# Graph attention, two layers on one core: the order of each layer's last scores, and rows requested in halves

## The chip, the cores and the metric

The kernel runs on one core of one Trainium2 chip. The metric is the device time of one execution in microseconds (us); lower is better. Before the change three runs took 2653.32 to 2656.51 us, with a median of 2653.38.

## The reference

The input is x (128 graphs, 64 nodes each, 768 features) and a 0/1 adjacency for each graph. Rows are normalised and rectified, and then go through two layers of graph attention, each with three 768 x 768 weights:

```python
m_left = jnp.einsum('bsh,oh->bso', h, W_left[l])
m_right = jnp.einsum('bsh,oh->bso', h, W_right[l])
u_left = jnp.einsum('bih,bjh->bij', h, m_left) / temper
u_right = jnp.einsum('bih,bjh->bij', h, m_right) / temper
u = u_left * adj_tri + u_left * diag_mask + u_right * jnp.swapaxes(adj_tri, 1, 2)
delta_exp_u = jnp.exp(u) * adj
attention = delta_exp_u / (jnp.sum(delta_exp_u, axis=2, keepdims=True) + 1e-10)
h_lin = jnp.einsum('bsh,oh->bso', h, W_lin[l]) + b_lin[l]
ctx = jnp.matmul(attention, h_lin)
h = jax.nn.relu(_layer_norm(ctx, ln_a[l], ln_b[l]))
```

After the second layer the input x is added. All of it is in float32.

## The kernel before

**Passes.** Each layer has two passes over all tokens. Pass one (`pass_one`, from L655) makes the attention and leaves it in DRAM; pass two (`pass_two`, from L1012) makes `h_lin`, the context and the norm. The texts below say "first layer" for l = 0 and "second layer" for l = 1.

**Blocks, parts, supers.** 512 tokens (8 graphs) are a block, 256 tokens a part. There are 16 blocks and 32 parts. `SUPER` (L172) groups the parts: a first super of two and then ten supers of three. A super's hidden states lie transposed in `HT`, one tile `ht` for each part: 128 partitions, `C` = 6 chunks of features, 256 tokens.

**Products.** From the second super on (in the second layer from the first), the left and right products of a super are made with a fast scheme of 40 products in place of 54: `PRODUCTS` (L116) names for each the sum of weights and the sum of tokens that enter. POOL makes the sums of tokens (class `Tokens`), DVE and POOL the sums of weights. A product is 8 recorded matmuls into one PSUM bank (C, D, X, Y, Z, V in rotation, four chains at a time). `READS` (L122) lists which outputs each product adds to, with its factor. The function `reads` (L904) issues these additions from the bank into the tiles `M` in SBUF: ACT for the first addition of an output, DVE for all others, the lines "m<-m,X" (L245) and L914 of the profile. There are 18 outputs. Output o belongs to part o // 6 of the super, to the left or right side (o // 3 % 2), and to the chunk pair o % 3 (chunks 0 and 1, 2 and 3, or 4 and 5). The last product, number 39, adds to the outputs 0, 4, 5, 6, 7 and 13. So outputs 0, 4 and 5 (part 0), 6 and 7 (part 1: left side, chunks 0 to 3) and 13 (part 2: left side, chunks 2 and 3) become final last.

**Scores.** `scores(k)` (L722) multiplies `ht` with `M` into the PSUM tile `sc`. For each of the super's six groups of two graphs (q; part q // 2) and each chunk c there are four matmuls, which the profile records twice each: 8 for each (q, c), 288 for a super. They are the line L733. Scores of super k - 1 are issued after the fourth product of super k (L925). Only the last super's scores have no products behind them: at the end of pass one (L936 to L947) the kernel issues the first step of the softmax (POOL), opens the banks of pass two's first groups 0, 1, 3 and 5 (`fresh`, with copies of the bias by ACT, L995), issues groups 0 and 1 (`multiply`, L1006), then the last scores, groups 3 and 5, and the softmax's next steps (`chain`, L737, which read the whole of `sc`). In the scores q runs outermost and c inside, so part 0 comes first.

**Memory shared across passes.** Pass two's tiles take the memory of pass one's. In the second layer parts 0 and 1 of `M` are one tile, and pass two's `a`, `b` (rows of the norm's weights) and its first `hl` (the output of groups) lie over it.

**The planner.** Python functions are put into a plan by slot (`put`, L67); a product is two slots, and `run` issues what is due in the middle and at the end of each product. What is planned is thus issued in order of slots on each engine's queue. `prepare(b, slot)` (L850) plans a block's rows in the first layer: four statistics at slots +1 to +7, the scale at +9, four norms (ACT, in place) at +11 to +17, four DVE transposes from the rows `x` to `xb` at +19, +21, +23 and +25 (L465), and at +27 the store of `xb` to DRAM by four DMAs on SP (L461, "h<-xb"). `end` is +28. There the next block's rows are requested (`load_rows`, L344, the DMAs "x<-in_x_dram" of L361): eight DMAs of 192 KB on SP into two tiles `x`, one for row groups 0 and 1 and one for 2 and 3. Behind them the `ht` loads of the block's two parts follow (L368), each held by a memset on DVE (L367) until the tile's earlier part is done with. Block 4's `prepare` begins at slot 118, so its store is at slot 145 and the request at 146; super 2's products begin at slot 152. In pass one of the second layer the rows come from DRAM where pass two of the first left them.

**SP's queue.** Stores, row requests, `ht` loads and the softmax's stores (L778) all go through SP in the order in which they are issued, and an instruction that waits holds those behind it. The adjacency goes through ACT's queue.

Of the kernel before, what the change touches and what calls it, by code (L numbers as in the profile page):

```python
# [17 lines left out]
def kernel(  # L18
# [12 lines left out]
    nc = tc.nc  # L31
    B, S, H = x.shape
    L = w_lin.shape[0]
    P = 128
    C = H // P
# [3 lines left out]
    PAIR = P // S  # L39
# [18 lines left out]
    PB = TH // S  # L58
# [8 lines left out]
    def put(slot, *fs):  # L67
        plan.setdefault(slot, []).extend(fs)

    def put_all(slot, fs, step=1):  # L70
        for f in fs:
            if f is not None:
                put(slot, f)
            slot += step
        return slot
# [5 lines left out]
    def run(slot):  # L81
# [34 lines left out]
    PRODUCTS = (  # L116
# [57 lines left out]
    PLAIN = 36  # L174
    SCORED = 3

    def begins(k, l=0):
        return 0 if k == 0 else 2 * (len(PRODUCTS) if l else PLAIN) + 2 * len(PRODUCTS) * (k - 1)

# [160 lines left out]
    XR = {}  # L340

    START = (0, 2, 1, 3)

    def load_rows(l, u, pool):  # L344

        XR[l, u] = []
        if (l, u) == (0, 0):

            rows = x.rearrange("(n k h) s f -> n k (h s) f", k=Q, h=PAIR)
            for g in range(2):  # L350
                t = pool.tile([P, 2, H], F32, name="x", bufs=2)
                XR[l, u].extend([t[:, 0, :], t[:, 1, :]])
            for q in START:
                nc.sync.dma_start(XR[l, u][q], rows[0, q])
            return
        for g in range(2):
            t = pool[g] if type(pool) is list else pool.tile([P, 2, H], F32, name="x", bufs=2)
            for a in range(4):
                i = 4 * g + a
                src = x[u * NBB + i] if l == 0 else ROWS[u][i]  # L360
                nc.sync.dma_start(t[a * 32:(a + 1) * 32], src.rearrange("(k j) h -> j k h", k=2))  # L361
            XR[l, u].extend([t[:, 0, :], t[:, 1, :]])

    def load_part(which, l, p, hold=False):
        ht = HT[which, l, p] = big.tile([P, C, TH], F32, name="ht", bufs=6)
        if hold:
            nc.vector.memset(ht[:, 0, :1], 0.0)  # L367
        nc.sync.dma_start(ht, KEPT[l][p])  # L368
# [5 lines left out]
    def affine_part(which, l, p, step=1):  # L374

        def part(c0):
            for c in range(c0, c0 + step):
                ht = HT[which, l, p][:, c, :]
                nc.scalar.activation(ht, ht, AF.Relu, bias=cols[1][:, c:c + 1], scale=cols[0][:, c:c + 1])  # L379

        return [lambda c=c: part(c) for c in range(0, C if l else 0, step)]
# [273 lines left out]
    def pass_one(l, start, final):  # L655
        with tc.tile_pool(name=f"one{l}", bufs=2, reuse_waits="tile") as sp, \
# [22 lines left out]
            if l:  # L679
                both = sp.tile([P, 2, C, PB, 2, S], F32, name="m", bufs=1)  # L680
                M = [both[:, 0], both[:, 1]]
                both = both.rearrange("p v c b k s -> p (v c b k s)").rearrange(
                    "p (c b k s) -> p c b k s", c=C, b=2 * PB, k=2)
# [25 lines left out]
            def out_of(bank, thirds=False, o=0):  # L709
                if thirds:  # L710
                    p = bank[:, :4 * CUT].rearrange("p (g b s) -> p g b s", g=2, s=WIDE)
                    return p[:, :, :, THIRDS[o // 6][1]:]
                return bank.rearrange("p (g b s) -> p g b s", g=2, s=S)
# [8 lines left out]
            def scores(k):  # L722
                nq = 2 * len(SUPER[k])
                p = KEEP["scores"].rearrange("p a (q m) -> p (a q) m", m=P)
                for q in range(nq):
                    ht, m = HT[1, l, SUPER[k][q // 2]], M[q // 2]
                    for c in range(C):
                        for h in range(PAIR):
                            b = q % 2 * PAIR + h
                            mb = both[:, c, q // 2 * PB + b] if l and k == 0 else m[:, c, b]  # L730
                            mb = mb.rearrange("p k j -> p (k j)")
                            for e in (0, 32):
                                nc.tensor.matmul(p[h * S + e:h * S + e + 32, q, e:e + 95],  # L733
                                                 ht[:, c, b * S + e:b * S + e + 32], mb[:, e:e + 95],
                                                 start=(c == 0), stop=(c == C - 1))

            def chain(k):  # L737
                adj, nq = ADJ[k], 2 * len(SUPER[k])
# [42 lines left out]
            def softmax(k):  # L781
                CHAIN[k] = chain(k)
                return [lambda: next(CHAIN[k], None)] * 8

            mid = None
            if l == 0:
# [5 lines left out]
                p = ps_st.tile([P, 2 * TH], F32, name="V")  # L792
# [6 lines left out]
                todo, turns = transpose_rows(0, 0, sp)  # L799
# [22 lines left out]
            def bank_of(n):  # L822
                n %= BANKS
                return KEEP["CD"][n] if n < 2 else KEEP["XYZV"[n - 2]]
# [25 lines left out]
            def prepare(b, slot, step=1):  # L850
                if (l, b) not in XR:
                    load_rows(l, b, sp)
                end = put_all(slot + 1, [f for f in transpose_rows(l, b, sp) if step > 1 or f is not None], 1)
                if b + 1 < NB and (l, b + 1) not in XR:
                    put(end + (8 if b == 2 else 0), lambda: load_rows(l, b + 1, sp))
                for t in range(2):
                    p = 2 * b + t
                    k = where[p][0]
                    before = p - 6
                    at = end + 3 + t  # L860
                    lag = 22 if b > 2 else 30 if l else 16
                    if before >= 0:
                        at = max(at, begins(where[before][0] + 1, l) + 2 * SCORED + 3)
                    put(at, lambda p=p, hold=before >= 0: load_part(1, l, p, hold))
                    put_all(at + lag + 6 * t, affine_part(1, l, p))
                    follow.setdefault(k, []).append(at + lag + (7 + 6 * t if l else 0))
                    if len(follow[k]) == len(SUPER[k]):
                        tokens.ready[k] = max(follow[k])
# [25 lines left out]
            last = len(SUPER) - 1  # L894
            for k in range(FIRST_OF[l], len(SUPER)):
                assert slot == begins(k, l)
                if k:
                    put_all(slot + 2 * SCORED + 4, softmax(k - 1), 3)
                    put(slot + 2 * SCORED + 42, lambda k=k: load_adj(k, nc.scalar))
                if k == last:  # L900
                    final(slot, tokens)
                seen, waiting = set(), []

                def reads(i):  # L904
                    for o, c in READS[i]:
                        bank = out_of(bank_of(CHAINS * (k - 1) + i % CHAINS), k == 0, o)
                        to = into(o, k == 0)
                        if o not in seen:
                            seen.add(o)
                            nc.scalar.activation(to, bank, AF.Copy, scale=float(c))  # L910
                        elif abs(c) == 1:
                            added(nc.vector, to, "+" if c > 0 else "-", to, bank)
                        else:
                            nc.vector.scalar_tensor_tensor(to, bank, float(c), to, op0=ALU.mult, op1=ALU.add)  # L914

                for i, (f, t) in enumerate(PRODUCTS):
                    while l and f not in weights.at:
                        fetch.popleft()()
                    w, tok = weights.need(f), tokens.need(k, t)
                    product(bank_of(CHAINS * (k - 1) + i % CHAINS), w, tok, i < CHAINS, slot, TH if k else 2 * CUT)  # L920
                    tokens.used(k, t)
                    if k == last:
                        weights.used(f)
                    waiting.append(i)
                    if i == SCORED and k:  # L925
                        scores(k - 1)
                    if i >= SCORED or k == 0:
                        for n in waiting:
                            reads(n)
                        waiting = []  # L930
                    turn_of(slot + 1)
                    slot += 2
# [432 lines left out]
```

## Time and profile before

| what | value |
|---|---|
| runs | 2653.32, 2653.38, 2656.51 us |
| the profiled execution's own time | 2651.07 us |
| its span, first to last instruction | 2649.3 us |
| mean granted TensorE clock | 0.995 |
| DVE busy | 1776.2 us (67%) |
| POOL busy | 1764.6 us (67%) |
| moved by DMA | 331.84 MB, mean 125 GB/s |
| code fetched for TensorE's queue (q8) | 145 packets, 2.38 MB |

The span is the time from the first to the last instruction; the execution's own time includes what lies around it. PE is TensorE's matmuls, PEld its weight loads, DVE VectorE, ACT ScalarE, POOL GpSimd and SP the engine that issues most DMAs. In a timeline a row gives start, length, engine, line, operation, output<-input, shapes and count, and in brackets the idle time ahead of it with what ended it. "issue" there means that the engine waited for nothing that the profile shows. The passes lie as follows: pass one of the first layer up to 860 us, pass two up to some 1340, pass one of the second layer up to 2158, pass two to the end.

### The profile page before, as it was taken

What the parts mean: (1) busy time and instruction counts of PE and PEld (TensorE: products, weight loads), DVE (VectorE), ACT (ScalarE), POOL (GpSimd) and SP (SyncE); (2) the same over time, 40 slices, a digit from 0 to 9 for tenths busy, and PEclk for the clock granted to TensorE, in tenths of its full rate; (3) what the DMA queues carried; (4) which work ended last, traced back from release to release, by engine and by line L of the source; (5) the groups of instructions that cost most, each with busy time, mean ns of one, the idle gap of its engine ahead of it and who ended that gap; (6) DMA issues with size and microseconds to landing.
All of it is one profiled execution on the core that took longest, in us unless ns stands there. A gap on an engine that the chain in (4) does not pass through costs nothing. (4 is left out here: it accounts for less than half of the span.)

```text
span 2649.3 us, 47197 instructions
## 1 busy us (share of the span) xinstructions
PE 2593.0 (98%) x18122; PEld 2216.7 (84%) x18122; DVE 1776.2 (67%) x2884; ACT 935.3 (35%) x1969; POOL 1764.6 (67%) x1396
## 2 busy tenths in 40 slices
PE   9899999999999999999999999999999999999998
PEld 8788888888888788888788888888888878888876
DVE  7877878777867445554446676677766676666667
ACT  5522123222213254454542222222222335555453
POOL 4766666656668657776266666667666657878786
PEclk9999999999999999999999999999999999999999
DMA  7443534343321344445794524353542215555555
GB/s 219 113 111 81 129 93 104 92 126 79 89 62 63 123 145 152 163 134 179 212 291 100 131 58 112 78 129 93 133 101 70 67 49 157 157 167 166 176 160 147
DMA packets 258465, 331.84 MB, mean 125 GB/s; under 512 B 56002, under 2 KB 190402, under 8 KB 258242
## 3 DMA queue, kind: packets, MB, share of 16 engines
q1 hardware_dynamic: 241442, 320.56, 44.1%
q10 hardware_dynamic: 16800, 8.26, 1.1%
q8 instruction: 145, 2.38, 0.4%
q14 instruction: 78, 0.64, 0.1%
HBM read 213.39 MB, written 115.34 MB: 124 GB/s over the span
## 5 line engine op out<-in xcount | busy, mean ns | idle before, releaser
L245 POOL TENSOR_TENSOR g<-ht 128x512 f32<-128x512 f32 (+1 forms) x620 | 785.4, 1278 | 424.3 <-PE X L702 82.1
L245 POOL TENSOR_TENSOR g<-g,g 128x512 f32<-128x512 f32 (+1 forms) x310 | 397.6, 1290 | 134.4 <-PE C L702 22.3
L245 POOL TENSOR_TENSOR g<-ht,g 128x512 f32<-128x512 f32 (+1 forms) x272 | 346.1, 1282 | 164.5 <-PE Z L702 43.9
L702 PE MATMUL X<-g,g 128*128 128x256 f32 (+1 forms) x1080 | 251.6, 376 | 2.5 <-POOL g L245 1.2
L702 PE MATMUL C<-g,g 128*128 128x256 f32 x1008 | 242.9, 384 | 9.2 <-POOL g L245 7.1
L1006 PE MATMUL Z<-g,g 128*128 128x256 f32 x1024 | 244.2, 380 | 3.8 <-ACT hl L300 3.6
L702 PE MATMUL Y<-g,g 128*128 128x256 f32 (+1 forms) x968 | 226.8, 377 | 4.4 <-POOL g L245 4.4
L702 PEld LDWEIGHTS X<-g,g 128*128 128x128 f32 x1080 | 201.5, 190 | 31.4 <-POOL g L245 2.5
L702 PEld LDWEIGHTS C<-g,g 128*128 128x128 f32 x1008 | 192.6, 192 | 38.0 <-issue 7.1
L1006 PEld LDWEIGHTS Z<-g,g 128*128 128x128 f32 x1024 | 191.6, 190 | 36.4 <-issue 4.1
L379 ACT ACTIVATE ht<-ht,b_col,a_col 128x256 f32<-128x256 f32 x384 | 196.1, 591 | 67.2 <-DMA ht<-h 42.5
L702 PE MATMUL Z<-g,g 128*128 128x256 f32 (+1 forms) x936 | 217.2, 375 | 0.0
L702 PE MATMUL D<-g,g 128*128 128x256 f32 x880 | 209.1, 381 | 0.6 <-POOL g L245 0.6
L702 PEld LDWEIGHTS Y<-g,g 128*128 128x128 f32 x968 | 182.7, 191 | 28.8 <-POOL g L245 4.8
L702 PE MATMUL V<-g,g 128*128 128x256 f32 (+1 forms) x840 | 193.8, 373 | 3.6 <-DVE m L245 2.0
L702 PEld LDWEIGHTS Z<-g,g 128*128 128x128 f32 x936 | 174.7, 190 | 23.2 <-issue 0.3
L702 PEld LDWEIGHTS D<-g,g 128*128 128x128 f32 x880 | 168.0, 191 | 24.7 <-POOL g L245 1.3
L1006 PE MATMUL X<-g,g 128*128 128x256 f32 x768 | 182.7, 379 | 0.0
L702 PEld LDWEIGHTS V<-g,g 128*128 128x128 f32 x840 | 156.9, 190 | 23.8 <-DVE m L245 2.2
L1206 POOL TENSOR_TENSOR z<-z,b 128x768 f32<-128x768 f32 x62 | 112.6, 1828 | 82.1 <-DVE z L1203 77.5
L245 DVE TENSOR_TENSOR m<-m,D 128x512 f32<-128x512 f32 x180 | 118.2, 677 | 70.5 <-ACT m L910 51.8
L245 DVE TENSOR_TENSOR m<-m,Y 128x512 f32<-128x512 f32 (+2 forms) x196 | 126.4, 666 | 57.9 <-ACT m L910 35.6
(222 smaller groups left out, 4607.8 us busy)
## 6 DMA issues: line engine op xcount, KB each, us to landing
ht<-h SPq DMA_DIRECT2D x126, 768.0 KB, 6.2
h<-xb SPq DMA_DIRECT2D x124, 384.0 KB, 7.0
z<-z SPq DMA_DIRECT2D x128, 192.0 KB, 3.1
x<-z SPq DMA_DIRECT2D x128, 192.0 KB, 5.3
xr<-in_x_dram SPq DMA_DIRECT2D x120, 192.0 KB, 3.8
out_dram<-xr SPq DMA_DIRECT2D x120, 192.0 KB, 2.7
x<-in_x_dram SPq DMA_DIRECT2D x112, 192.0 KB, 5.4
g<-form SPq DMA_DIRECT2D x40, 256.0 KB, 5.1
```

Of the source, the lines that this page charges most:

```text
L245: (eng.tensor_add if sign == "+" else eng.tensor_sub)(o, a, b)
L379: nc.scalar.activation(ht, ht, AF.Relu, bias=cols[1][:, c:c + 1], scale=cols[0][:, c:c + 1])
L702: nc.tensor.matmul(o, w[:, c, g * P:(g + 1) * P], t, start=(new and g == c == at == 0), stop=(c == K2 - 1), skip_group_check=True)
L1006: nc.tensor.matmul(p[:, n], b[t][:, c, r * P:(r + 1) * P], w[s][:, c, :], start=(i in FIRST and i not in PRELOAD and n == c == 0), stop=(c ...
L1206: nc.gpsimd.tensor_add(zs[k], zs[k], rows["b"])
```

## The change

First, where k is the last super, `scores` goes through its (q, c) pairs in the order of a new table `SCORES_LAST`: part 2 with chunks 0, 1, 4, 5; part 1 with 4, 5; part 2 with 2, 3; part 1 with 0 to 3; part 0 with all. As sums of several q are then open in one bank, only the first matmul to a bank and a group of its partitions has the start flag. Second, `reads` of the last super's last product takes its outputs in the order 13, 6, 7, 0, 4, 5 (`LAST_READ`). For other supers the order of scores is the old one. Third, in the first layer `load_rows` for blocks 4 to 15 is called twice: for tile 0 at `end - 5`, which is slot +23, behind the third transpose, and for tile 1 at `end`.

```diff
+    SCORES_LAST = ((2, (0, 1, 4, 5)), (1, (4, 5)), (2, (2, 3)), (1, (0, 1, 2, 3)), (0, tuple(range(C))))
+    LAST_READ = (13, 6, 7, 0, 4, 5)
...
-    def load_rows(l, u, pool):
+    def load_rows(l, u, pool, some=range(2)):
...
-        for g in range(2):
+        for g in some:
...
-                for q in range(nq):
+                todo, begun, left = [(q, c) for q in range(nq) for c in range(C)], set(), {}
+                if k == last:
+                    todo.sort(key=lambda qc: next(n for n, (v, cs) in enumerate(SCORES_LAST)
+                                                  if qc[0] // 2 == v and qc[1] in cs))
+                for q, c in todo:
                     ht, m = HT[1, l, SUPER[k][q // 2]], M[q // 2]
...
+                    left[q] = left.get(q, C) - 1
...
+                            new = (q // 4, h, e) not in begun if k == last else left[q] == C - 1
+                            begun.add((q // 4, h, e))
+                            nc.tensor.matmul(p[h * S + e:h * S + e + 32, q, e:e + 95],
+                                             ht[:, c, b * S + e:b * S + e + 32], mb[:, e:e + 95],
+                                             start=new, stop=not left[q], skip_group_check=k == last)
...
-                    put(end + (8 if b == 2 else 0), lambda: load_rows(l, b + 1, sp))
+                    if l == 0 and b > 2:
+                        put(end - 5, lambda: load_rows(l, b + 1, sp, (0,)))
+                        put(end, lambda: load_rows(l, b + 1, sp, (1,)))
+                    else:
+                        put(end + (8 if b == 2 else 0), lambda: load_rows(l, b + 1, sp))
...
-                    for o, c in READS[i]:
+                    at_end = k == last and i == len(PRODUCTS) - 1
+                    for o, c in sorted(READS[i], key=lambda oc: LAST_READ.index(oc[0])) if at_end else READS[i]:
```

More of the change, by code (lines that the diff above doesn't have):

```diff
@@ L342 @@
     START = (0, 2, 1, 3)
-    def load_rows(l, u, pool):
-        XR[l, u] = []
+    def load_rows(l, u, pool, some=range(2)):
+        XR.setdefault((l, u), [])
         if (l, u) == (0, 0):
@@ L724, in scores @@
                 p = KEEP["scores"].rearrange("p a (q m) -> p (a q) m", m=P)
-                for q in range(nq):
-                    ht, m = HT[1, l, SUPER[k][q // 2]], M[q // 2]
[L727 to L735, printed above, removed]
+                todo, begun, left = [(q, c) for q in range(nq) for c in range(C)], set(), {}
[3 more added lines that the diff above has]
+                for q, c in todo:
+                    ht, m = HT[1, l, SUPER[k][q // 2]], M[q // 2]
+                    left[q] = left.get(q, C) - 1
+                    for h in range(PAIR):
+                        b = q % 2 * PAIR + h
+                        mb = both[:, c, q // 2 * PB + b] if l and k == 0 else m[:, c, b]
+                        mb = mb.rearrange("p k j -> p (k j)")
+                        for e in (0, 32):
+                            new = (q // 4, h, e) not in begun if k == last else left[q] == C - 1
[3 more added lines that the diff above has]
+                                             start=new, stop=not left[q], skip_group_check=k == last)
             def chain(k):
```

## The prediction

> **What bounds the kernel now.** I read the page first, then the waits of TensorE, then the timeline of the places which the change touches.
>
> ```profile
> span 2649.3 us, 47197 instructions
> PE 2593.0 (98%) x18122; PEld 2216.7 (84%) x18122; DVE 1776.2 (67%) x2884; ACT 935.3 (35%) x1969; POOL 1764.6 (67%) x1396
> ```
>
> TensorE is busy for 2593.0 of 2649.3 us. A change that leaves its matmuls alone, as this one does, can save only some of the 56.3 us in which it stands, and time in which it runs slowly. The waits of TensorE from 95 to 790 us, which is the first layer's pass one after its start, have three lines, and those of POOL in the same stretch include one on `ht`:
>
> ```profile
> PE sc L733 <- issue: 5.6, 6, 2.7
> PE sc L733 <- DVE m L245: 2.4, 4, 1.2
> PE C L702 <- ACT m L910: 1.0, 1, 1.0
> ```
> ```profile
> POOL g L245 <- DMA ht<-h: 36.5, 4, 11.4
> ```
>
> Columns: total, times, longest. So almost every stop is inside the score matmuls (`sc`), and most of it is "issue": nothing in the profile is awaited. The measure for a score block that nothing disturbs, between two products:
>
> ```profile
> 324.49 1.89 PE L702 MATMUL Y<-g,g 128*128 128x256 f32 x8
> 326.31 6.31 PE L733 MATMUL sc<-m,ht 128*32 128x95 f32 x288
> 332.55 1.99 PE L702 MATMUL C<-g,g 128*128 128x256 f32 x8
> ```
>
> The scores start 1.82 us after the start of the group ahead of them, and the next group starts 6.24 us later: 21.7 ns for each of 288 recorded matmuls (two for each in the code).
>
> **Part A, the last scores, first layer.** Timeline:
>
> ```profile
> 861.86 1.89 PE L1006 MATMUL V<-g,g 128*128 128x256 f32 x8
> 864.16 2.47 DVE L245 TENSOR_TENSOR m<-m,Y 128x512 f32<-128x512 f32 x4
> 864.89 6.32 PE L733 MATMUL sc<-m,ht 128*32 128x95 f32 x265 [1.14 <-DVE m L245]
> 865.49 0.32 PEld L733 LDWEIGHTS sc<-m,ht 128*32 128x32 f32 x16 [0.28 <-DVE m L245]
> 866.09 4.95 PEld L733 LDWEIGHTS sc<-m,ht 128*32 128x32 f32 x234 [0.28 <-DVE m L245]
> 866.55 0.68 DVE L914 SCALAR_TENSOR_TENSOR m<-Y,m 128x512 f32<-128x512 f32 x1
> 867.15 0.67 DVE L245 TENSOR_TENSOR m<-m,Y 128x512 f32<-128x512 f32 x1
> 867.94 0.59 ACT L995 COPY Y<-g 128x512 f32<-128x512 f32 x1 [3.02 <-DVE m L245]
> 871.85 0.69 PE L733 MATMUL sc<-m,ht 128*32 128x95 f32 x23 [0.64 <-issue]
> 872.47 1.99 PE L1006 MATMUL X<-g,g 128*128 128x256 f32 x8
> ```
>
> DVE adds the last product's six outputs from 864.16 to 867.82, one each 0.6 us, in the order 0, 4, 5, 6, 7, 13. The scores begin with part 0, which needs output 0 at once, 4 sixteen matmuls later and 5 after sixteen more: hence 1.14 and twice 0.28 us.
>
> The change removes no instruction and adds none. In the new order 64 matmuls (part 2, chunks 0, 1, 4, 5) and 32 (part 1, chunks 4, 5) need none of these six outputs, so they can start at 861.86 + 1.82 = 863.68, 1.21 us earlier. Then 13 is wanted at 863.68 + 96 x 0.0217 = 865.76 and is there at 864.83; 6 at 866.46 (865.5), 7 at 866.8 (866.1), 0 at 867.85 (866.7), 4 at 868.2 (867.3), 5 at 868.55 (867.82). The least margin is 0.7 us: no wait on DVE is left. If only that counted, the block would end at 863.68 + 6.24 = 869.92 for 872.47: 2.55 us, the upper bound.
>
> What is late next is "issue". The 0.64 us stop falls after matmul 265. Each matmul has a weight load, so 128 of them are 256 instructions, and stops of this kind in one block lie 128 matmuls apart (second layer: 158 and 286, below). I take them for code that arrives in blocks, each asked for when the block before it is entered. Matmul 137 ran at 866.09 + 105 x 0.0217 = 868.37, and the block after it could go on at 871.85: 3.48 us, against 128 x 0.0217 = 2.78 us that the matmuls need. With the earlier start, matmul 9 runs at 863.88 and 137 then 2.78 to 3.28 us later (3.28 is what it took before, waits included), at 866.66 to 867.16; matmul 265 at 870.14 to 870.64; the next group 0.62 us later, at 870.76 to 871.26. Gain 1.2 to 1.7; I take 1.2, as the code supply had just these gaps.
>
> [...]
>
> **Part A, second layer.**
>
> ```profile
> 2160.19 1.89 PE L1006 MATMUL V<-g,g 128*128 128x256 f32 x8
> 2163.22 4.01 PE L733 MATMUL sc<-m,ht 128*32 128x95 f32 x158 [1.14 <-DVE m L245]
> 2164.42 2.60 PEld L733 LDWEIGHTS sc<-m,ht 128*32 128x32 f32 x126 [0.28 <-DVE m L245]
> 2167.39 2.82 PE L733 MATMUL sc<-m,ht 128*32 128x95 f32 x128 [0.15 <-issue]
> 2170.86 0.35 PE L733 MATMUL sc<-m,ht 128*32 128x95 f32 x2 [0.66 <-issue]
> 2171.14 1.99 PE L1006 MATMUL X<-g,g 128*128 128x256 f32 x8
> ```
>
> Start at 2162.01. Matmul 30 ran at 2164.1, 158 at 2167.39 (3.27 us), 286 at 2170.86 (3.47 us). Now 30 runs at 2162.66, 158 at 2165.93, 286 at 2169.4, the next group at 2169.68: gain 1.46, say 1.5. Without the code limit 2162.01 + 6.24 = 2168.25: 2.9.
>
> Here part 0 shares its memory with tiles that the next pass writes, so the first copies into `hl` and the loads of `a` and `b` must now wait for the end of the scores. These copies (two of some 0.6 us) lie beside the two groups of 1.73 us that follow the scores: no cost, and at most 1.2 us if that cover were gone. The bias copy into Y (867.94 above) still follows the last addition and is 2 us ahead of its group. DVE's softmax begins at the end of the scores as before and moves with it.
>
> Part A: 1.2 + 1.5 = **2.7 us**. From above 2.55 + 2.9 = 5.4; from below nothing, should refills take 0.7 us longer each.
>
> **Part B, rows in two halves.** Twelve requests are split (rows of blocks 4 to 15). I looked at each score block of the first layer for the traffic beside it. One meets rows:
>
> ```profile
> 169.12 4.60 PE L733 MATMUL sc<-m,ht 128*32 128x95 f32 x211
> 176.45 3.32 PE L733 MATMUL sc<-m,ht 128*32 128x95 f32 x77 [2.73 <-issue]
> 179.69 2.19 PE L702 MATMUL Z<-g,g 128*128 128x256 f32 x8
> 181.72 1.89 PE L702 MATMUL V<-g,g 128*128 128x256 f32 x8
> ```
> ```profile
> 157.40 5.15 SPq L461 DMA_DIRECT2D h<-xb  x4
> 162.66 6.84 SPq L361 DMA_DIRECT2D x<-in_x_dram  x8
> ```
> ```profile
> 170.00:174.00 4.00, 3.72 (x179) 3.51 (x170) 0.00 (x0) 1.01 (x3) 0.62 (x1) 1.00 0.98 215
> 176.40:179.70 3.30, 3.25 (x78) 2.91 (x77) 0.00 (x0) 0.00 (x0) 0.00 (x0) 0.55 0.02 5
> ```
>
> The last three columns of the windows are granted clock, DMA share, GB/s. From scores to next group it is 10.57 us here for 6.24: 4.33 lost, of which 2.73 is the stop, and the rest a granted clock of 0.55 after it. The following group takes 2.03 for 1.82: another 0.2. DMA was full up to about 174 with block 4's store and block 5's rows. The code block is in the DMA queues' rows: none from 170 to 173.5, where the data queue is alone, one after that:
>
> ```profile
> q1 hardware_dynamic: 328, 0.81, 103.7%
> ```
> ```profile
> q8 instruction: 1, 0.02, 2.8%
> ```
>
> Its request belongs to matmul 83, at 169.12 + 83 x 0.0217 = 170.9. Code came 5.5 us later, not 3.48.
>
> With the change the first half is issued at slot 141, between transposes. Its tile is free after the second one:
>
> ```profile
> 152.90 0.96 DVE L465 STREAM_TRANSPOSE xb<-x 128x768 f32<-128x768 f32 x1
> ```
>
> So SP issues four requests of 0.855 us (6.84 / 8) from 153.9 to 157.3, ahead of the store at 157.40, which isn't delayed. The rows total 8 x 192 KB; half of them, 0.79 MB at 215 GB/s, is 3.7 us of traffic, moved into a time when SP had issued nothing. DMA then drains at about 170.5, before the code is asked for at 170.9. Code comes at 170.9 + 3.48 = 174.4; natural arrival at matmul 211 is 173.7, so a stop of 0.7 stays, like the 0.64 us above, after which no slow stretch follows. The 77 matmuls take 77 x 0.0217 + 0.14 = 1.8 us: next group at 176.2 for 179.69, 3.5 us, and 0.1 to 0.2 from its speed: **3.6 us**. Bounds: 4.5 (all of it) and nothing.
>
> The other eleven splits I cost at nothing. Each moves four requests past the store of the block's transposed part, and past a softmax's stores where these are near; those come at most 3.4 us later, and the `ht` loads behind them up to 3.4 us earlier. What covers this is POOL's lead: TensorE waited for no POOL sum from 95 to 790 us. Without cover it is the slower rival below. The remaining stops of "issue" there, 5.6 - 2.7 = 2.9 us, bound a further gain; they have no rows beside them, so I take none.
>
> **Sum.** 2.7 + 3.6 = 6.3 us. The profiled execution took 2651.07 us (span 2649.3): 2644.8. The median shown is 2653.38, 2.3 us above it; I forecast against that: **2647.1 us**.
>
> **Rivals.**
>
> *The code block doesn't wait for rows.* If a refill gets its turn between packets, the 2.7 us stop has another cause, and only part A remains: 2653.38 - 2.7 = 2650.7. For it: refill stops of 0.64 and 0.66 us also come with no rows near (the two ends above). Against: the refill packet appears just as the data ends. 0.17. [...]
>
> *Code is no limit.* Both upper bounds: 5.4 + 4.5 = 9.9, 2643.5. Against: 3.3 to 3.5 us per block in both layers. 0.08.
>
> *Part A does not do what it says.* If waits are for whole parts, the scores still start with the first addition (864.89) and stand again for part 1; only the two 0.28 stay, about 1 us in both layers: 2653.38 - 1 - 3.6 = 2648.8. Against: the old order waited chunk by chunk. 0.06.
>
> *Slower: SP held by the early half.* Its request stands at the head of SP's queue until DVE has done two transposes; behind it wait the block's store and its `ht` loads, then POOL's sums, which already waited four times for `ht`. From the point where POOL's lead is under the delay (up to 3.4 us), TensorE stops, and a long stop also slows what follows:
>
> ```profile
> 844.56 2.61 PE L702 MATMUL C<-g,g 128*128 128x256 f32 x8 [2.52 <-POOL g L245]
> 846.97 2.97 PE L702 MATMUL D<-g,g 128*128 128x256 f32 x8
> 849.77 1.89 PE L702 MATMUL X<-g,g 128*128 128x256 f32 x8
> ```
>
> Two groups take 5.21 us for 3.45, with the wait 4.3 us lost. Three such stops in twelve blocks: 12.9 - 6.3 = 6.6 us slower, 2660. Against: no wait for POOL in that stretch. 0.07.
>
> **How the numbers follow.** My forecast has 0.62. A measurement can tell 0.2%, 5.3 us, from no change; the forecast's 6.3 lies just beyond, with some 1.2 us either way from the refill times and the drain, so I give 0.48 of it to faster and 0.14 to same. With the rivals: faster 0.48 + 0.08 = 0.56; same 0.14 + 0.17 + 0.06 = 0.37; slower 0.07. The range runs from the case without code limit, 2643.5, to the case of part A alone with 0.8 us for a worse refill, 2651.5; the slower case is left out.
>
> **What would show it.** Right: no wait on DVE before either last score block, and those blocks 1 to 2 us nearer to the group ahead; in each still one stop of "issue" of 0.6 to 1 us; the stop in the block at 169 us under 1 us, the granted clock 1.0 behind it, and rows drained before 171 us. Wrong: that stop still above 2 us though the rows are gone; a wait of TensorE for POOL or `ht` between 95 and 790 us; new waits of TensorE on `hl` after the last scores.

## The result, and the profile after

Four runs of the changed kernel took 2640.21 to 2644.4 us, with a median of 2642.6; four of the kernel before, on the same chip, 2653.32 to 2657.48, median 2654.95. The ratio is 0.9953, with a 95% interval of 0.9941 to 0.9964: 12.35 us faster by the medians, where 6.3 was forecast. The time is 0.9 us below the range on record. A second comparison on another chip (e4 below) gives 0.9967 [0.9955, 0.998], 9.9 us. The two profiled executions are 7.1 us apart, 2651.07 and 2643.98 us; single runs of one kernel scatter by about 2.5 us (standard deviation).

The head of the page after, and then what TensorE waited for from 95 to 790 us:

```profile
span 2642.2 us, 47249 instructions
PE 2590.5 (98%) x18122; PEld 2216.3 (84%) x18122; DVE 1776.0 (67%) x2884; ACT 934.9 (35%) x1969; POOL 1764.3 (67%) x1396
```
```profile
PE sc L743 <- issue: 3.2, 6, 1.2
PE sc L743 <- DVE m L248: 1.2, 4, 0.3
```

The matmuls are the same 18122. In this stretch "issue" fell from 5.6 to 3.2 us (e3, the kernel before again, has 6.8), and the waits of the scores on DVE from 2.4 to 1.2. TensorE still waits for no POOL sum there.

**The block at 169 us.** TensorE's timeline, SP's queue, and windows (columns as in the prediction: the last three are granted clock, DMA share, GB/s):

```profile
168.75 1.89 PE L705 MATMUL D<-g,g 128*128 128x256 f32 x8
170.57 6.47 PE L743 MATMUL sc<-m,ht 128*32 128x95 f32 x288
176.97 1.99 PE L705 MATMUL Z<-g,g 128*128 128x256 f32 x8
```
```profile
155.34 1.74 SPq L364 DMA_DIRECT2D x<-in_x_dram  x4
158.85 5.17 SPq L464 DMA_DIRECT2D h<-xb  x4
164.12 4.95 SPq L364 DMA_DIRECT2D x<-in_x_dram  x4
```
```profile
168.00:170.50 2.50, 2.50 (x13) 1.98 (x11) 2.50 (x5) 0.00 (x0) 1.89 (x2) 1.00 0.91 244
170.50:174.00 3.50, 3.50 (x169) 3.43 (x172) 0.76 (x2) 0.00 (x0) 1.28 (x1) 1.00 0.33 88
174.00:177.00 3.00, 3.00 (x133) 2.63 (x121) 0.47 (x1) 2.56 (x5) 0.00 (x0) 1.00 0.03 8
```

Four requests now stand ahead of the store and four behind it. DMA is down to a third of its time once the scores run, all 288 matmuls go in one row without a stop, and the clock stays at 1.00. The scores start 1.82 us after the group ahead and the next group 6.40 us later: 0.16 us lost, where it was 4.33.

**The last scores of the first layer, and of the second:**

```profile
857.46 1.89 PE L1021 MATMUL V<-g,g 128*128 128x256 f32 x8
859.28 6.28 PE L743 MATMUL sc<-m,ht 128*32 128x95 f32 x288
865.49 1.99 PE L1021 MATMUL X<-g,g 128*128 128x256 f32 x8
```
```profile
2155.17 1.89 PE L1021 MATMUL V<-g,g 128*128 128x256 f32 x8
2156.99 6.19 PE L743 MATMUL sc<-m,ht 128*32 128x95 f32 x286
2164.11 0.35 PE L743 MATMUL sc<-m,ht 128*32 128x95 f32 x2 [0.93 <-issue]
2164.39 1.99 PE L1021 MATMUL X<-g,g 128*128 128x256 f32 x8
```

No wait on DVE is left in either. The first has no stop of "issue" either; the second keeps one of 0.93 us at matmul 286.

**Where the 7.1 us lie.** I cut both traces at the same matmuls and took the difference of each stretch, after less before: the block at 169 us and the group behind it -4.4; the rest of the first layer's pass one up to its last scores -1.5; these last scores -2.6; the second layer's last scores -1.7; its pass two -0.3. Together -10.5. The other stretches gave +3.4 back (start to 169 us +1.4, the end of the first layer's pass two +1.1, the second layer's pass one up to its last scores +0.8). The 1.4 us lie ahead of 93 us, before the first split request is issued (115.96), the change doesn't touch the work of the other two, and the two profiles of the kernel before (the first and e3) differ from each other by 1.0 and 3.2 us there. Another difference between executions is the clock: up to the last matmul it was granted at 0.50 for 17.1 us before, 23.9 in e3, 13.7 after and 17.1 in e4, in pieces of 3.41 us or multiples. In one such piece TensorE loses up to 1.7 us, half of 3.41.

For the experiments I use one measure: what a score block loses against the undisturbed one of the prediction, that is, the time from the start of the group ahead to the start of the group behind, less 1.82 + 6.24 us. In us, from one profiled execution of each:

| kernel | block at 169 us | other 8, layer one | last, layer one | last, layer two |
|---|---|---|---|---|
| before | 4.33 | 9.08 | 2.55 | 2.89 |
| e3, before again | 4.45 | 10.41 | 2.64 | 3.15 |
| after | 0.16 | 7.64 | -0.03 | 1.16 |
| e4, after again | 0.22 | 9.13 | 0.62 | 1.78 |
| e1, part A alone | 2.77 | 10.14 | 0.30 | 1.53 |
| e2, part B alone | 0.70 | 7.30 | 2.55 | 2.79 |
| e5, one split | 0.64 | 8.66 | 2.48 | 2.95 |
| e6, the other eleven | 2.46 | 8.85 | 2.67 | 3.90 |
| e7, block 5's rows late | 0.47 | 9.92 | 2.54 | 3.44 |
| e8, code shifted | 2.90 | 8.15 | 1.85 | 2.06 |
| e9, order of scores alone | 3.44 | 10.46 | 3.68 | 3.67 |
| e10, order of reads alone | 4.49 | 9.90 | 5.18 | 5.56 |
| e12, after with shift | 0.00 | 5.65 | 0.17 | 0.36 |

### The profile page after: what moved, and what is told of

Read it like the earlier page. It is cut to its first block, busy times and chain, and to the rows that moved or that the text cites. A ratio compares the mean times of both kernels' runs of the same rounds, so it can differ in the third digit from the quotient of the medians.

```text
span 2642.2 us, 47249 instructions
## 1 busy us (share of the span) xinstructions
PE 2590.5 (98%) x18122; PEld 2216.3 (84%) x18122; DVE 1776.0 (67%) x2884; ACT 934.9 (35%) x1969; POOL 1764.3 (67%) x1396
## 4 chain that ended last, share of the span: by engine, by line
PE 86%; DVE 5%; DMA 3%; ACT 2%; issue 1%; POOL 1%; SPq 1%; ACTq 0%; DVEq 0%; POOLq 0%
PE Z L1021 12%; PE C L705 8%; PE Y L705 8%; PE X L705 8%; PE D L705 8%; PE Y L1021 8%; PE Z L705 8%; PE V L705 7%; PE X L1021 6%; PE sc L743 5%; PE V L1021 4%; PE aux L1063 2%; DVE m L248 2%; POOL g L248 1%; DMA g<-form 1%
```

## The experiments

My theory was that of the prediction: the block at 169 us stops because its code waits behind rows, and the last blocks because they wait for DVE and then for code. Rivals: the refill doesn't wait for rows; the excess over the forecast comes from the other eleven splits, or from scatter.

**e1 to e4: the parts alone, and both kernels again.** Runs on one chip, beside 27 runs of the kernel before (median 2652.97, 2649.76 to 2659.08). e1 undoes the split:

```diff
-                    if l == 0 and b > 2:
-                        put(end - 5, lambda: load_rows(l, b + 1, sp, (0,)))
-                        put(end, lambda: load_rows(l, b + 1, sp, (1,)))
-                    else:
-                        put(end + (8 if b == 2 else 0), lambda: load_rows(l, b + 1, sp))
+                    put(end + (8 if b == 2 else 0), lambda: load_rows(l, b + 1, sp))
```

> Part A alone (the order of the last scores and of the last reads), rows requested whole as before. Theory 1 (the two traces: each last score block loses its waits on DVE, and the stop of the code refill gets shorter too, because a refill is no longer asked for late behind a waiting matmul): 4 to 5 us faster than before, 2.6 in the first layer and 2.1 in the second; no wait of TensorE on DVE at either last score block. Theory 2 (my prediction: the code supply keeps its gaps): 2.7 us faster. Theory 3 (the larger gain is run-to-run difference in the stretches that the change does not touch): under 2 us. The stop of 2.7 us in the score block at about 169 us stays in all three.

e2 undoes the order of scores and of reads:

```diff
-                if k == last:
+                if False:
...
-                            new = (q // 4, h, e) not in begun if k == last else left[q] == C - 1
+                            new = left[q] == C - 1
...
-                    at_end = k == last and i == len(PRODUCTS) - 1
+                    at_end = False
```

> Part B alone (rows of blocks 4 to 15 in two halves), scores and reads in the old order. Theory 1: 4.4 us faster, all of it in the score block at about 169 us, whose stop and slow clock go; the last score blocks keep their waits on DVE of 1.14 us and twice 0.28 us. Theory 2 (the other eleven splits help too, as the trace after has shorter stops in the blocks at 250, 403 and 558 us): 6 to 7 us faster. Theory 3 (a refill does not wait for rows): no change, and the stop at 169 us stays.

e3 and e4 are the kernels before and after, without an edit.

> The kernel before, unchanged, for a second profile. All theories: no change in time. What tells them apart: if the stops of 0.6, 0.9 and 1.25 us in the score blocks at 250, 403 and 558 us, the 2.0 us wait at 77 us and the stops at 1356 and 1396 us come back within 0.2 us, they are fixed for this program, and the differences there between before and after belong to the change; if they move by 0.5 us and more, they are differences from run to run. The stop of 2.7 us at 169 us should come back in any case.

> The changed kernel, unchanged, for a second profile and a time on this chip. Theory 1: 9 us faster than before (4.5 from part A, 4.4 from part B), equal to the sum of the two single parts within 1.5 us. Theory 2: 12 us, more than the sum of the parts. In its profile no stop over 0.5 us in the score block at about 170 us, and no wait on DVE at the last score blocks.

Measured: e1 2649.29 us (11 runs), ratio 0.9992 [0.9983, 1.0001], which doesn't exclude no change; e2 2649.71 (11), 0.9984 [0.9975, 0.9992]; e3 2654.02 (11), 1.0002 [0.9994, 1.0011]; e4 2643.09 (5), 0.9967 [0.9955, 0.998]. By means, with standard errors, e1 saves 3.3 +- 1.0 us, e2 4.5 +- 0.9, e4 9.9 +- 1.2. The parts make 7.8; that they are worth 2.1 more together is within these errors. By time alone e1 can't tell 2.7 from 4 us, nor e2 4.4 from 6; the traces have to. The first comparison's 12.35, with four runs a side, is at the high end of the same gain.

In the table each part acts where it was meant to: e1 on the two last blocks, e2 on the block at 169 us. e1's last block, first layer:

```profile
862.26 5.66 PE L743 MATMUL sc<-m,ht 128*32 128x95 f32 x265
868.18 0.69 PE L743 MATMUL sc<-m,ht 128*32 128x95 f32 x23 [0.26 <-issue]
```

The stop is at matmul 265 as before, but 0.26 us for 0.64. It varies between executions of the new order, from nothing (after) to 0.62 lost (e4).

**e5 to e7: whose rows stop the block at 169 us.** All without part A, on one chip, beside 30 runs of the kernel before (2654.09). e5 splits block 5's rows alone, e6 all but those, and e7 is the kernel before with block 5's rows requested 24 slots later, behind the scores:

```diff
# e5
-                    if l == 0 and b > 2:
+                    if l == 0 and b == 4:
# e6
-                    if l == 0 and b > 2:
+                    if l == 0 and b > 2 and b != 4:
# e7
-                    put(end + (8 if b == 2 else 0), lambda: load_rows(l, b + 1, sp))
+                    put(end + (8 if b == 2 else 24 if l == 0 and b == 4 else 0), lambda: load_rows(l, b + 1, sp))
```

> Only the request of block 5's rows (the one beside the score block at 169 us) in two halves; the other eleven and all of part A as before. Theory 1 (three sources of the gain: that score block 3.7 us, the last scores 3.8 us, the other eleven splits about 2 us): the score block at 169 us loses its 2 to 4 us, and nothing else changes: 3 to 4 us faster than before. Theory 2 (my prediction costed the other splits rightly at nothing): this run is as fast as part B alone, 4.5 us.

> The other eleven requests in two halves, block 5's whole, part A as before. Theory 1: the score block at 169 us keeps its stop of 2.6 us or more; the waits on DVE before the score blocks at 403 and 558 us shrink from 0.6 and 1.2 us to 0 and 0.3, because the loads of ht behind the rows come 3.4 us earlier, POOL's sums start earlier, and a small DVE operation in the norm (nb) no longer stands behind a POOL operation of 1.27 us there (1.19 us for 0.24); 1 to 2 us faster in all. Theory 2: no change.

> The kernel before with one edit: block 5's rows requested whole, but 24 slots later (behind the score block at 169 us), so that no rows move while its code is fetched. Theory 1 (the refill waited for the rows): the stop of 2.7 us falls under 1 us, about 3.5 us faster in that block, as with the halves. Rival (a refill does not wait for rows; the halves helped in another way, by the earlier store and ht loads): the stop stays at 2.6 us or more.

Measured: e5 2647.19 us (6 runs), 0.9971 [0.9959, 0.9983]; e6 2652.26 (12), 0.9991 [0.9982, 1.0]; e7 2654.83 (11), 0.9999 [0.999, 1.0009]. The block in e5, e6 and e7:

```profile
171.94 4.60 PE L743 MATMUL sc<-m,ht 128*32 128x95 f32 x211
176.97 1.92 PE L743 MATMUL sc<-m,ht 128*32 128x95 f32 x77 [0.44 <-issue]
```
```profile
168.95 4.60 PE L743 MATMUL sc<-m,ht 128*32 128x95 f32 x211
175.81 1.92 PE L743 MATMUL sc<-m,ht 128*32 128x95 f32 x77 [2.26 <-issue]
```
```profile
170.13 4.60 PE L733 MATMUL sc<-m,ht 128*32 128x95 f32 x211
174.99 1.92 PE L733 MATMUL sc<-m,ht 128*32 128x95 f32 x77 [0.26 <-issue]
```

The same matmul, 211, in all three. With block 5's rows in halves the stop is 0.44 us, with them out of the way altogether 0.26, with them whole 2.26, though the other eleven requests are split. The code's packet shows it too: it begins 4.1 to 5.0 us after the scores' first matmul in the six profiles of unshifted code with these rows whole, 2.2 to 2.6 in the five with them in halves or late. And in all 14 profiles each of the 211 stops of "issue" in the scores ends 2.1 to 3.0 us after the start of a packet of code. So the stops are code, and the rival that a refill doesn't wait for rows falls by the 2.26 against 0.26 us.

e7 saved 3.9 us in this block and gave them back. DVE's waits from 180 to 300 us, TensorE's from 180 to 600, and SP's queue:

```profile
DVE st L336 <- DMA x<-in_x_dram: 5.0, 2, 3.5
```
```profile
PE V L702 <- POOL g L245: 1.4, 1, 1.4
```
```profile
180.58 35.39 SPq L361 DMA_DIRECT2D x<-in_x_dram  x16
```

DVE stands for the rows, and TensorE then for POOL: from the second group behind this block to the end of the stop at 844 us the kernel needs 668.9 us, where the eleven other profiles whose code isn't shifted have 661.3 to 664.3. The edit did more than it was meant to: there are 16 requests in place of 8, since block 5's preparation found no rows and asked as well. So e7 shows that a free block isn't enough if rows come late and SP is held, but not what a late request alone costs.

e5 saves more by its runs, 6.9 +- 1.0 us, than its block does (3.7 in the profile). e5 and e6 together are e2, and their 6.9 + 2.6 on this chip stand against 4.5 +- 0.9 on the other. What the rest is stays open.

**e8: where the stops lie.** The kernel before with 24 transposes more behind the 34 at the start (L793); they compute nothing that is used:

```diff
-                for _ in range(34):
+                for _ in range(58):
```

> The kernel before with 24 more warm-up transposes, which do nothing for the output, at the very start: all later code lies 24 matmuls (48 instructions) further, so blocks of code end 24 matmuls earlier in the program. Theory 1 (the stops called issue are refills of code, and a refill asked for behind a matmul that waits comes late): the stops in all score blocks move 24 matmuls earlier (at the first layer's end from 265 to 241), and there the refill is now asked for ahead of the matmul that waits on DVE, so the stop of 0.64 us after the waits goes and the loss in that block falls from 2.55 to about 1.9 us. Rival (my prediction: blocks of code come at fixed gaps of 3.5 us): the stop moves too, but stays at 0.6 us. Rival 2 (not code): the stops stay at matmul 211, 229 and 265 of their blocks.

Measured: 2649.09 us (8 runs), 0.9983 [0.9972, 0.9995]. The block at 169 us, then the first layer's last block:

```profile
170.23 4.11 PE L733 MATMUL sc<-m,ht 128*32 128x95 f32 x187
177.11 2.32 PE L733 MATMUL sc<-m,ht 128*32 128x95 f32 x101 [2.78 <-issue]
```
```profile
860.61 1.89 PE L1006 MATMUL V<-g,g 128*128 128x256 f32 x8
863.65 6.95 PE L733 MATMUL sc<-m,ht 128*32 128x95 f32 x288 [1.14 <-DVE m L245]
870.52 1.78 PE L1006 MATMUL X<-g,g 128*128 128x256 f32 x7
```

The stop moves from matmul 211 to 187, by exactly the 24 instruction pairs put in: these stops belong to places in the code. It is 2.78 us long here too, behind the same rows. In the last block the stop is gone and the waits on DVE are not, and the loss falls from 2.55 to 1.85: the two are separate costs. Where all of the 5.0 us by which the medians differ come from isn't shown: e8's profile has 8.5 us of "issue" in the scores, the first one before 8.1 and e3 12.8.

**e9 and e10: the halves of part A,** both with whole requests; e9 keeps the old order of reads, e10 the old order of scores (its edits to `scores` are those of e2).

```diff
# e9
-                    at_end = k == last and i == len(PRODUCTS) - 1
+                    at_end = False
# e10
-                if k == last:
+                if False:
```

> Half of part A: the new order of the last scores, the last product's reads in the old order (0, 4, 5, 6, 7, 13), rows whole. Both theories take the order of reads for needed: output 13, now wanted after 96 matmuls, is still the last to be added, 3.7 us after the first addition begins. The scores start 1.2 us earlier and then stand about 2 us for DVE; the last score blocks lose about 2.1 to 2.4 us each, where the old order loses 2.6 and 3.0: at most 1 us faster in all. If the gain of part A came from the scores' order alone, it would be 3.8 us.

> The other half: the last reads in the order 13, 6, 7, 0, 4, 5, the scores in the old order, part 0 first, rows whole. Output 0 comes 1.85 us later than before, and the scores begin with it: each of the last two score blocks starts 1.85 us later and loses about 4 us and more; 3 to 4 us slower than before in all. Rival (the order of reads does not matter): no change.

Measured, beside 21 runs of the kernel before (2653.84): e9 2655.17 us (10 runs), 1.0001 [0.999, 1.0011]; e10 2657.65 (10), 1.0016 [1.0007, 1.0025]. The last block in e9, then in e10:

```profile
865.51 2.17 PE L743 MATMUL sc<-m,ht 128*32 128x95 f32 x96
869.72 5.78 PE L743 MATMUL sc<-m,ht 128*32 128x95 f32 x192 [2.04 <-DVE m L248]
```
```profile
867.12 8.28 PE L743 MATMUL sc<-m,ht 128*32 128x95 f32 x288 [3.13 <-DVE m L248]
```

In e9 the 96 matmuls that need no late output start at once, as the prediction said, and then the scores stand 2.04 us for output 13, which the old order adds last. In e10 the scores stand 3.13 us at once, since output 0 is now added fourth. Neither half gains alone. For e9 2.1 to 2.4 us of loss were expected in these blocks; 3.7 came. There is no stop of code in them; the rest is the clock behind the wait (e9, third last column):

```profile
871.00:874.00 3.00, 3.00 (x85) 3.00 (x80) 0.00 (x0) 0.38 (x1) 0.00 (x0) 0.50 0.00 0
```

It was granted at 0.50 for 3.41 us, and at 0.50 in e10's last blocks too, where the wait is longer still; the waits of 1.14 us in the kernel before are followed by none.

**e11 and e12: two ways to more.** e11 cuts every score block but the last, and that behind the second layer's first super, in two: `scores(k, qs)` makes half of the groups after product 3, with the reads of products 0 and 1 behind them, and the others after product 4. e12 is the changed kernel with e8's 24 transposes.

```diff
# e11
-                        scores(k - 1)
+                            scores(k - 1, (2, 3, 0))
...
+                    if i == SCORED + 1 and k and not (l and k == 1):
+                        scores(k - 1, (1, 4, 5)[:2 * len(SUPER[k - 1]) - 3])
# e12
-                for _ in range(34):
+                for _ in range(58):
```

> The changed kernel, and the scores of every super but the last (and but the first of the second layer) in two pieces of 144 recorded matmuls with one product between them: groups 2, 3, 0, then product 4, then groups 1, 4, 5. Theory 1 (the stops called issue are code refills of about 3.5 us for blocks that 128 score matmuls use up in 2.8): the product gives a refill 1.7 us more, so nearly all stops of issue in these 18 blocks go, 6 to 9 us in sum over the profile; product 4 may wait some 0.2 to 0.3 us each time for ACT's first copies; 3 to 6 us faster than the changed kernel. Rival (not the code supply): the stops stay, and the waits for ACT make it 3 us or more slower than the changed kernel.

> The changed kernel with 24 more warm-up transposes, which do nothing for the output. Theory 1: as in the kernel before, the code blocks end 24 matmuls earlier, which there took 2 to 3 us from the stops of issue and the waits behind them; the changed kernel has lost part of these already, so 1 to 3 us faster than the changed kernel. Rival (the 5 us that the shift gave before came from the start, not from the score blocks): the sum of the losses in the 20 score blocks is as in the changed kernel.

Measured, beside the same 21 runs: e11 2642.88 us (5 runs), 0.9955 [0.9941, 0.9969]; e12 2639.53 (5), 0.9945 [0.9933, 0.9957]. TensorE's waits in the whole profile, of after, of e11 and of e12:

```profile
PE sc L743 <- issue: 6.8, 14, 1.2
```
```profile
PE sc L743 <- DVE m L248: 8.4, 4, 2.1
...
PE sc L743 <- issue: 0.9, 1, 0.9
```
```profile
PE sc L743 <- issue: 4.2, 12, 0.7
```

e11 does away with nearly all stops of code, 6.8 to 0.9 us, and pays 8.4 us of new waits for them, most likely since the scores of part 1 come first now and its outputs 6 and 7 are added late. The 3 to 6 us over the changed kernel that I expected didn't come. e12 is the fastest kernel here, 14.3 us ahead of before by the medians. The losses of its 20 full score blocks add up to 9.6 us, against 12.3 in after and 16.0 in e4: the shift acts there, and not at the start alone. That e12 also beats the change by some 2 to 4 us is likely but not settled: their ratios come from different chips, and the intervals overlap.

## Why the prediction was right or wrong

**Direction and places: right.** Every term of the sum acts where it was put. The sum was too small: 6.3 for 9.9 +- 1.2 us in the larger comparison. The profiles' averages below make 3.1 + 2.3 + 1.7 + 1.7 + 0.3 = 9.1: two terms were too small, part A in the first layer by 1.1 us and the other eleven splits, put at nothing.

**Part B at 169 us, 3.6 us: right, its last part by luck.** Four kernels with this split lose 0.43 us on average in this block (e2, after, e4, e5), seven with whole requests 3.55 (before, e3, e1, e6, e8, e9, e10): 3.1 us. Between the two profiles on record it is 4.2. That the stop comes with rows beside it is shown by e5 to e7: 0.44 us with these rows in halves, 2.26 whole, 0.26 late. But the slow clock behind the stop, which the sum took for certain, isn't: four of the seven have it and lose 3.4 to 4.5 us (before, e3, e9, e10), three haven't and lose 2.5 to 2.9 (e1, e6, e8). The forecast stop of 0.7 us was 0.44 in e5 and none in after. The four early requests took 1.74 us in place of 3.4.

**Part A, second layer, 1.5 us: right.** On average 3.19 in six profiles without part A (before, e3, e2, e5, e6, e7), 1.49 in three with it (after, e4, e1): 1.7 us. The stop at matmul 286 stayed, 0.93 us, and the groups behind waited 1.5 us on `hl`, as before.

**Part A, first layer, 1.2 us: wrong in size, 2.3 measured** (2.57 without, 0.30 with, the same profiles). The step that failed is "I take 1.2, as the code supply had just these gaps". Those gaps of 3.3 to 3.5 us belong to code that itself came late. The queue of code (packets, MB, share) before, from 865.0 to 866.0 us, and after, from 856.6 to 859.28:

```profile
q8 instruction: 1, 0.02, 6.4%
```
```profile
q8 instruction: 1, 0.02, 2.8%
```

Before, the packet for this block comes 1.05 us after the scores' first matmul (864.89); after, 2.67 us ahead of it (859.28). This holds for each profile: 0.87 to 1.57 us behind it in the seven that have the old order of scores and the old place in the code (before, e3, e2, e5, e6, e7, e10), 2.0 to 2.7 ahead in the four with the new (after, e4, e1, e9). In e8, where the end of a block of code lies ahead of the matmul that waits for DVE, the wait stayed and the stop went. So the request for code most likely stands behind that matmul. This is an estimate from the packets, as is the prediction's idea that a block is asked for when the one before it is entered: requests themselves are not in the traces. Against the group ahead the packet comes 4.9 us earlier, for a start of the scores that is 1.21 us earlier. Why so much, the runs don't show. Take the wait away, and code comes earlier too; 2.3 is near the upper bound of 2.55, and the stop that I kept is 0 to 0.6 us. Why the request behind it, that of matmul 137, varies (its packet comes 1.1 us after that matmul before, 0.4 in after and e1, 1.0 in e4), and with it what is left of the stop, the runs don't show.

**"The other eleven splits I cost at nothing": most likely wrong, by some 1.7 us.** From the second group behind the block at 169 us to the end of the stop at 844 us, five profiles with whole requests (before, e3, e1, e9, e10) take 663.8 us on average and four with these splits (e2, after, e4, e6) 662.1. The size isn't certain: e5, where these eleven are whole too, takes 662.5. e6 has just these splits, with 2.6 +- 1.0 us by its runs. The prediction named their effect, earlier `ht` loads, and covered it with POOL's lead; but a POOL that starts earlier has an effect of its own. POOL's wait for `ht`, before and after:

```profile
541.83 1.27 POOL L245 TENSOR_TENSOR g<-ht 128x512 f32<-128x512 f32 x1 [11.44 <-DMA ht<-h]
```
```profile
534.05 1.27 POOL L248 TENSOR_TENSOR g<-ht 128x512 f32<-128x512 f32 x1 [7.70 <-DMA ht<-h]
```

POOL is then some 3.7 us further on, and a small DVE operation ahead of a score block meets only the end of a POOL operation. Before, then after:

```profile
555.96 1.27 POOL L245 TENSOR_TENSOR g<-ht 128x512 f32<-128x512 f32 x1
556.06 1.19 DVE L406 SCALAR_TENSOR_TENSOR nb<-mv,rs 128x4 f32<-128x4 f32 x1
```
```profile
550.97 1.27 POOL L248 TENSOR_TENSOR g<-ht 128x512 f32<-128x512 f32 x1 [0.39 <-PE X L705]
552.02 0.23 DVE L409 SCALAR_TENSOR_TENSOR nb<-mv,rs 128x4 f32<-128x4 f32 x1
```

The operation on 128x4 takes 1.19 us when it begins beside a POOL operation and ends with it, 0.23 us when it begins as POOL's is about to end. Ahead of this block it ends, in 13 profiles (all but e11), within 0.03 us of the end of a POOL operation. That one microsecond is seen in the score block behind it, before and after:

```profile
557.90 4.33 PE L733 MATMUL sc<-m,ht 128*32 128x95 f32 x175 [1.25 <-DVE m L245]
```
```profile
552.91 4.34 PE L743 MATMUL sc<-m,ht 128*32 128x95 f32 x175 [0.30 <-DVE m L248]
```

The operation's time and this wait go together: 1.21 and 1.27 us in e1, 0.78 and 0.84 in e3, 0.45 and 0.52 in e9, and 0.23 to 0.24 and 0.30 in e2, e6 and after. It isn't these splits alone that do it: e5 has 0.23 and 0.29 without them. At the block at 403 us, though, the operation takes 0.23 to 0.24 us in the five profiles with these splits (after, e2, e4, e6, e12) and 0.42 to 1.10 in the eight with them whole. Between before and after the block at 558 us is worth 0.95 us of wait and the one at 403 us 0.28; what makes the rest of the 1.7 isn't shown. Why the small operation ends with POOL's, the runs don't show.

**The base.** I forecast against one median of three runs. With a scatter of 2.5 us that median is uncertain by more than 1 us, and the comparison's own median before was 2654.95. The range had no term for this, and none for a gain in the eleven splits. Its lower end was the rival "code is no limit".

**The rivals.** "The code block doesn't wait for rows" fell with e5 to e7 (2.26 us of stop with these rows whole, 0.26 with them late). "Part A does not do what it says" fell: the scores start 1.82 us after the group ahead, with no wait. "SP held by the early half" fell: four requests took 1.74 us at 155.34, the store went at 158.85, and TensorE waited for no POOL sum. "Code is no limit" has a price of 9.9 us, which is e4's gain, but that is chance: it came true for after in the first layer's two blocks, and the second layer's stop of 0.93 us speaks against it.

Open: 0.34 us in pass two of the second layer, which takes 467.32 to 467.33 us from the group behind the last scores to the last matmul in all profiles with whole requests, and 466.98 to 466.99 in all with any split; and why e5's runs gain more than its block.

## What to carry to other kernels

A stop that the profile calls "issue" in dense small matmuls can be code that comes late: look for stops a fixed count of instructions apart (here 128 pairs), for a packet of code that begins shortly before each stop ends (here 2.1 to 3.0 us), and at what fills the DMA queues when the code is due (here rows: 2.26 us of stop with them whole, 0.26 with them late). If a wait is taken away, don't carry over the refill times of the profile before, as the request for code may stand behind that wait (here the packet came 1.05 us after the scores' first matmul before, 2.67 us ahead of it after). Don't count a slow clock behind a stop as certain, either: with whole rows it was there in four profiles of the block at 169 us and not in three. And when work is reordered to suit when outputs become final, the producer's order and the consumer's must be changed together: either alone gained nothing or lost 0.16%.

## What the runs showed of the hardware

- Code for TensorE comes in blocks: stops in one score block lie 128 pairs of weight load and matmul apart (158 and 286). In dense scores 128 pairs take 2.78 us (128 x 21.7 ns), and the stops add up to 8.1 us before, 12.8 in e3 and 6.8 in after. TensorE goes on 2.1 to 3.0 us after the start of the code's packet (211 stops, 14 profiles). 24 unused transposes at the start moved the stop at 169 us from matmul 211 to 187, and the kernel was 5.0 us faster (e8).
- The DVE operation on 128x4 (`nb<-mv,rs`, L406) takes 0.16 us at its shortest (before, at 37.52 us). Ahead of the block at 558 us it takes as long as the POOL operation of 1.27 us beside it still runs: 1.19 us before, 0.23 after, 1.21 in e1.
- A slow stretch of TensorE after a stop isn't certain. Where there is one here, the granted clock is 0.50 for 3.41 us or a multiple: e3, a second profile of the kernel before, has two such pieces more than the first, e9 five. After the 2.52 us stop at 844 us, which the prediction shows, two groups took 5.21 us. In e5 the same stop is followed by 3.53 us for two groups:

```profile
843.14 1.97 PE L705 MATMUL C<-g,g 128*128 128x256 f32 x8 [2.51 <-DVE m L248]
844.94 1.89 PE L705 MATMUL D<-g,g 128*128 128x256 f32 x8
846.67 1.89 PE L705 MATMUL X<-g,g 128*128 128x256 f32 x8
```

e1, e7 and e12 look like e5; the other ten have the slow stretch. So like executions differ by this too.
